# A graph layer's edge loop: constants in a PSUM bank, one-hots on ScalarE, four engines ordered by hand, and a start and end shared differently

## The chip, the cores and the metric

One core of a Trainium2 chip runs the whole program. Its engines work side by side, each through its own list of instructions, and wait for each other by semaphores: TensorE (PE in the profile; its weight loads are PEld), VectorE (DVE), ScalarE (ACT), GpSimd (POOL) and SyncE (SP), which here only issues transfers. The metric is the device time of one execution in microseconds. The profile is of one execution, whose time is given beside its span.

## The reference

A layer of a graph network on 12,500 nodes of 32 features and 400,000 edges, which come sorted by their destination `dst`:

```python
h = jnp.maximum(_layernorm(x), 0.0)                          # 12500 x 32
e_feat = jnp.concatenate([h[src], h[dst], edge_attr], -1)     # 400000 x 96
v = jax.nn.relu(e_feat @ W1 + b1) @ W2 + b2                   # 96 -> 64 -> 32
out = x + jnp.maximum(segment_max(v, dst, 12500), h)
```

The layer norm divides by `sqrt(var + 1e-5)` and has no weights. The sources are random, so `h[src]` is a true gather of 400,000 rows of 128 bytes; the destinations are sorted, so consecutive edges mostly share theirs.

## The kernel before

**Start.** Partition p holds nodes 98p to 98p+97 (`NT` is 98). `x` is normalized in four pieces of 28, 28, 28 and 14 nodes per partition (L155 to L174), reductions and scaling on VectorE, squares and roots on ScalarE, and `h` is stored to `h_d` in DRAM (L174). From `h` come also `hs` (L209, L210), its value in two parts for TensorE, and the table `q_d`, h times the destination part of W1 (L222 to L232). A stage named "windows" (L236 to L268) works out for each edge whether it is the last of its destination (`at`), and a flag for inputs that the fast path can't take (then the code from L433 on runs; it doesn't here).

**The loop.** The edges lie in four stripes of 196 chunks of 512. The loop (L363 on; 98 iterations) takes two chunks of all four stripes, a *pair*, at a time. Per pair:

- *Sources.* A chunk needs `h[src]` for 16 blocks of 128 edges. Twelve are fetched by GpSimd with one indirect DMA each (L143). Four (`MM`) are made on TensorE, in *tiles*: VectorE builds one-hot matrices `hot` and `its` from keys (L285, L287); 15 matmuls (L292, L295) select the rows, with a large negative penalty on all but the wanted one of 14 nodes; VectorE's max-reduction (L297) takes it into `gm`. Chunks 0, 1 and 195 have no tiles and are gathered whole. `to_features` (L324, L326) transposes both kinds into `ht`. The tiles come from a generator, one per `next(tiles)`, one pair ahead of their use.
- *Hidden layer.* Four PSUM banks `ph0` to `ph3`, one per stripe, sum up three products (L379): of the edge attributes `ea`, of the destination part, and of `ht` with w1a. The destination part is a window `qw` of 32 rows of `q_d`, loaded from the chunk's first destination on, times a one-hot `of` that VectorE builds from the destinations (L370). ScalarE's relu gives `hid` (L389).
- *Output and maximum.* w2 (L399) puts two chunks into two `pv` banks; VectorE's scan (L404) runs the maximum along the edges, reset by penalties `pb` where the destination changes. In the *leave* of a chunk, `leave_1` transposes the scan (L336), adds b2 (`so`, L338) and marks the last edge of each destination (`last`, L340); `leave_2` brings these edges' values into node order by matmul (L350), ScalarE copies them (`wo`, L353), and SyncE stores them to `top_d` (L357).

**Banks and buffers.** PSUM: `ph0` to `ph3`, `tr` for the leaves, and three `pv` banks, which the tiles and w2 share in turn. Gathered chunks have six buffers, so GpSimd may run three pairs ahead: the gathers of a pair wait until the transposes of the pair three before have freed its buffers.

**Order.** In the loop SyncE and TensorE follow the order of the code; VectorE, ScalarE and GpSimd are ordered by a scheduler, which places the transposes into `ht` of the next pair ahead of the rest of the present one: in the trace L324 stands, one iteration early, after the reduction of the present iteration's first tile.

**End.** Both `top_d` and `h` are loaded, the maximum and the sum with `x` are taken in four pieces (L423 to L429, L507, L508) and stored.

Of the kernel before, what the change touches and what calls it, by code (L numbers as in the profile page):

```python
# [20 lines left out]
DVE = mybir.EngineType.DVE  # L21

# [21 lines left out]
MMC = range(2, NCH - 1)  # L44
AHEAD = 2
PIECE = 2 * A0
ROUND = 12582912.0
# [11 lines left out]
def gnn_kernel(ctx, tc, x, src, src_mm, src_t, dst, dst_next, dst_ext, lo, hi, edge_attr, weights, w1, w2, b2, out):  # L59
# [41 lines left out]
    lo_i = const.tile([1, NS, NCH], I32, name="lo_i")  # L101
    nc.sync.dma_start(lo_i, lo.rearrange("(o s) c -> o s c", o=1))
# [6 lines left out]
    node = const.tile([P, NCH], F32, name="node")  # L109
    for s in range(NS):  # L110
        nc.gpsimd.iota(node[s * W:(s + 1) * W], pattern=[[0, NCH]], base=0, channel_multiplier=1,
                       allow_small_or_imprecise_dtypes=True)
# [36 lines left out]
    with tc.tile_pool(name="nodes", bufs=1) as pool, tc.tile_pool(name="nodes_ps", bufs=2, space=PSUM) as ps:  # L149
# [4 lines left out]
        sts = [pool.tile([P, 2, PIECE], F32, name=f"st{k}") for k in range(len(pieces))]  # L154
        with tc.manual_schedule(engines={DVE, SP}):  # L155
            for st, r in zip(sts, pieces):
                n = r.stop - r.start
                nc.vector.tensor_reduce(st[:, 0, :n], xs[:, r], axis=AX.X, op=ALU.add)
                nc.vector.tensor_scalar(st[:, 0, :n], st[:, 0, :n], 1.0 / D, None, op0=ALU.mult)
                nc.vector.tensor_tensor(h[:, r], xs[:, r], st[:, 0, :n, None].to_broadcast([P, n, D]),  # L160
                                        op=ALU.subtract)
                nc.scalar.activation(sq[:, r], h[:, r], AF.Square)
            for st, r in zip(sts, pieces):
                n = r.stop - r.start
                nc.vector.tensor_reduce(st[:, 1, :n], sq[:, r], axis=AX.X, op=ALU.add)
                nc.vector.tensor_scalar(st[:, 1, :n], st[:, 1, :n], 1.0 / D, EPS, op0=ALU.mult, op1=ALU.add)
                nc.scalar.activation(st[:, 0, :n], st[:, 1, :n], AF.Sqrt)
            for st, r in zip(sts, pieces):
                n = r.stop - r.start
                nc.vector.reciprocal(st[:, 1, :n], st[:, 0, :n])  # L170
                nc.vector.scalar_tensor_tensor(h[:, r], h[:, r], 0.0,
                                               st[:, 1, :n, None].to_broadcast([P, n, D]),
                                               op0=ALU.max, op1=ALU.mult)
                nc.sync.dma_start(h_v[:, r], h[:, r])  # L174
# [39 lines left out]
        nc.vector.tensor_tensor(node, node, lo_w, op=ALU.add)  # L214
# [57 lines left out]
    with tc.tile_pool(name="edges", bufs=3) as pool, tc.tile_pool(name="edges_ps", bufs=1, space=PSUM) as ps, \  # L272
            tc.manual_schedule(engines={SP, PE}):
        loaded = {}
        windows = {}
        mm_rows = {}

        def rows_by_matmul():

            for i, c in enumerate(MMC):  # L280
                kb = pool.tile([P, 2, MM * P], F16, name="kb", bufs=2)
                nc.scalar.dma_start(kb, ap(key_d, i * MM * P, [[0, P], [len(MMC) * MM * P, 2], [1, MM * P]]))
                hot = pool.tile([P, A1, MM * P], F32R, name="hot", bufs=2)
                for k in range(A1):
                    nc.vector.tensor_scalar(hot[:, k], kb[:, 0], key_p[:, k:k + 1], None, op0=ALU.is_equal)  # L285
                its = pool.tile([P, MM * P], BF16, name="its", bufs=2)
                nc.vector.tensor_scalar(its, kb[:, 1], place, None, op0=ALU.is_equal)  # L287
                gm = mm_rows[c] = pool.tile([P, MM, D], F32, name="gm", bufs=6)
                for m in range(MM):
                    e = slice(m * P, (m + 1) * P)  # L290
                    po = ps.tile([P, C], F32, name="pv", bufs=3)[:, :D * A0]
                    nc.tensor.matmul(po, its[:, e], others.rearrange("p f a -> p (f a)"), start=True, stop=False)  # L292
                    for k in range(A1):
                        for part in range(2):
                            nc.tensor.matmul(po, hot[:, k, e], hs[:, part, k].rearrange("p f a -> p (f a)"),  # L295
                                             start=False, stop=(k == A1 - 1 and part == 1))
                    nc.vector.tensor_reduce(gm[:, m, :], po.rearrange("p (f a) -> p f a", a=A0),  # L297
                                            axis=AX.X, op=ALU.max)
                    yield

        def load(c):
            if c % LOAD == 0:
# [5 lines left out]
                for s in range(NS):  # L308
                    g = slice(s * D, (s + 1) * D)
                    nc.scalar.dma_start(db[g, :n], ap(dst_ext, 1 + s * S + c * C, [[0, D], [1, n]]))  # L310
                    nc.scalar.dma_start(pb[g, :n], ap(pen_d, s * S + c * C, [[0, D], [1, n]]))
                for k in range(c, min(c + LOAD, NCH)):
                    loaded[k] = [t[:, (k - c) * C:(k - c + 1) * C] for t in (ea, db, pb)]
            _, base = nc.values_load_multi_w_load_instructions(
                lo_i[0:1, :, c], engines=[SP], min_val=0, max_val=N)
            qw = pool.tile([P, HID], F32, name="qw", bufs=6)
            for s in range(NS):
                nc.sync.dma_start(qw[s * W:(s + 1) * W, :], q_d[bass.ds(base[s], W), :])
            windows[c] = qw, base
# [11 lines left out]

        def leave_1(c, sm):

            px = ps.tile([P, J, P], F32, name="tr")
            for j in range(J):
# [3 lines left out]
            last = pool.tile([P, J, NS, W], F32, name="last", bufs=2)  # L339
            nc.vector.tensor_tensor(  # L340
                last, iota_w[:, None, None, :].to_broadcast([P, J, NS, W]),
                at[:, :, c * J:(c + 1) * J].rearrange("p s j -> p j s")[:, :, :, None].to_broadcast([P, J, NS, W]),
                op=ALU.is_equal)
            return so, last

        def leave_2(c, so, last):

            pw = ps.tile([P, J, P], F32, name="tr")[:, 0]
            for j in range(J):
                nc.tensor.matmul(pw, last[:, j].rearrange("p s w -> p (s w)"), so[:, j, :],  # L350
                                 start=(j == 0), stop=(j == J - 1))
            wo = pool.tile([P, P], F32, name="wo")
            nc.scalar.activation(wo, pw, AF.Copy)  # L353
            _, base = windows.pop(c)
            for s in range(NS):
                g = slice(s * W, (s + 1) * W)
                nc.sync.dma_start(top_d[s % 2][bass.ds(base[s], W), :], wo[g, s * D:(s + 1) * D])  # L357

        tiles = rows_by_matmul()
        for c in range(AHEAD):  # L360
            load(c)
        sm = None
        for c in range(0, NCH, 2):  # L363
            for k in range(c + AHEAD, min(c + AHEAD + 2, NCH)):
                load(k)
            gh = [gather(c + x) for x in range(2)]
            of = []
            for x in range(2):
                of.append(pool.tile([P, C], F32, name="of", bufs=4))
                nc.vector.tensor_scalar(of[x], loaded[c + x][1], node[:, c + x:c + x + 1], None, op0=ALU.is_equal)  # L370


            ph = [ps.tile([P, C], F32, name=f"ph{s}") for s in range(NS)]

            def into_ph(pairs, start, stop):
                for s in range(NS):
                    g = slice(s * D, (s + 1) * D)
                    for x, (w, e) in enumerate(pairs):
                        nc.tensor.matmul(ph[s][x * HID:(x + 1) * HID], w[g], e[g], start=start, stop=stop)  # L379

            into_ph([(w1c, loaded[c + x][0]) for x in range(2)], True, False)
            into_ph([(windows[c + x][0], of[x]) for x in range(2)], False, False)
            next(tiles, None)
            ht = [to_features(c + x, gh[x]) for x in range(2)]
            into_ph([(w1a, ht[x]) for x in range(2)], False, True)
# [4 lines left out]
            next(tiles, None)  # L390
            next(tiles, None)

            if c > 0:
                left = leave_1(c - 1, sm)
            pv = [ps.tile([P, C], F32, name="pv", bufs=3) for x in range(2)]
            for s in range(NS):
                for x in range(2):
                    g = slice(x * HID, (x + 1) * HID)
                    nc.tensor.matmul(pv[x][s * D:(s + 1) * D], w2x[g], hid[s][g], start=True, stop=True)  # L399
            sms = []  # L400
            for x in range(2):
                before = -LOW if sm is None else sm[:, C - 1:C]
                sm = pool.tile([P, C], F32, name="sm", bufs=4)
                nc.vector.tensor_tensor_scan(sm, loaded.pop(c + x)[2], pv[x], before, op0=ALU.add, op1=ALU.max)  # L404
                sms.append(sm)
            next(tiles, None)
            next(tiles, None)
            if c > 0:
                leave_2(c - 1, *left)
            next(tiles, None)  # L410
            left = leave_1(c, sms[0])
            next(tiles, None)
            leave_2(c, *left)
# [157 lines left out]
```

## Time and profile before

| what | value |
|---|---|
| median of three runs (lowest, highest) | 5231.67 us (5231.43, 5264.13) |
| profiled execution: time, span | 5227.3 us, 5225.5 us |
| mean granted TensorE clock | 0.81 |
| busy: TensorE, its weight loads, VectorE, ScalarE, GpSimd | 70%, 53%, 35%, 6%, 43% |
| gathers (L143) | 2353, of 950 ns each |
| tile matmuls (L292, L295), reductions (L297) | 772 + 10808, 772 of 623 ns |
| first gather, first w2, last w2's end, end | 29.7, 232.8, 5184.9, 5225.5 us |

How to read it: an engine's busy time is only of its work on data; its waiting is given as idle time ahead of an instruction, with the last to release it ("<-DVE ht L324" means that VectorE's instruction of line 324, which writes `ht`, ended the wait; "issue" means that nothing which the profile shows was waited for, and "remote" a signal of another engine). A group's row has the count, the busy time in sum, the mean of one in nanoseconds, and the idle time. A shape such as 128x448 is partitions by elements. A window's row gives the busy time of each engine within a stretch of the span, the number of instructions, and the granted clock as a share of full speed.

### The profile page before, as it was taken

To read this page: it belongs to the slowest core of one execution; us is meant where nothing else is said; L and a number is where in the kernel's file an instruction comes from. 1 tells how busy PE (TensorE), PEld (TensorE's weight loads), DVE (VectorE), ACT (ScalarE), POOL (GpSimd) and SP (SyncE) were. 2 spreads that over 40 slices of the span, in tenths; PEclk is the share of its full clock that TensorE was granted. 3 is DMA by queue.
4 is the path that set the end of the run, shared out by engine and by line. 5 is a ranking of instruction groups with operands and counts; after the bars stand their busy time and mean duration, and the time that the engine had idled before them with its cause. 6 is when DMAs were issued, how large, how long until landed. Compare 5 with 4: busy or idle time off the path is not lost. (4 is left out here: it accounts for less than half of the span.)

```text
span 5225.5 us, 57318 instructions
## 1 busy us (share of the span) xinstructions
PE 3638.2 (70%) x20281; PEld 2775.9 (53%) x20281; DVE 1846.3 (35%) x3612; ACT 315.6 (6%) x627; POOL 2238.9 (43%) x2369
## 2 busy tenths in 40 slices
PE   2376767676767676767676767676767676777687
PEld 1255555555555555555554555555555555555565
DVE  2333333333333333333333333333333333333344
ACT  1000000000000000000000000000000000000000
POOL 6534344444444444444444444444444444444420
PEclk6587878787878787878788888787878787878788
DMA  3321112211211121112111211121112211211121
GB/s 123 90 58 43 42 39 58 44 41 40 58 42 41 40 56 44 40 40 56 44 40 40 57 44 40 40 56 44 41 40 57 44 41 40 57 44 40 40 53 65
DMA packets 235577, 256.47 MB, mean 49 GB/s; under 512 B 123653, under 2 KB 211861, under 8 KB 222102
## 3 DMA queue, kind: packets, MB, share of 16 engines
q10 hardware_dynamic: 74084, 137.60, 9.7%
q0 software_dynamic: 75296, 38.70, 5.6%
q1 hardware_dynamic: 85906, 76.48, 4.9%
q8 instruction: 159, 2.61, 0.2%
q14 instruction: 132, 1.08, 0.1%
HBM read 238.44 MB, written 14.04 MB: 48 GB/s over the span
## 5 line engine op out<-in xcount | busy, mean ns | idle before, releaser
L143 POOL DMA_INDIRECT gh<-h_d,src_i x2353 | 2234.8, 950 | 2812.1 <-DVE ht L324 2098.3
L295 PE MATMUL pv<-hs,hot 128*128 128x448 f32 x10808 | 2874.0, 413 | 712.6 <-issue 712.4
L295 PEld LDWEIGHTS pv<-hs,hot 128*128 128x128 f32 x10808 | 2282.8, 212 | 1444.9 <-issue 1270.9
L297 DVE TENSOR_REDUCE gm<-pv 128x32 f32<-128x448 f32 x772 | 481.2, 623 | 2548.3 <-remote 1529.4
L292 PE MATMUL pv<-others,its 128*128 128x448 bf16 x772 | 301.9, 391 | 427.0 <-issue 386.0
L285 DVE TENSOR_SCALAR hot<-kb,key_p 128x512 fp32r<-128x512 f16 x1351 | 555.8, 479 | 9.5 <-DMA qw<-q_d 9.5
L350 PE MATMUL tr<-so,last 128*128 128x128 f32 x1568 | 250.2, 282 | 250.0 <-issue 240.8
L404 DVE TENSOR_TENSOR_SCAN sm<-pb,sm,pv 128x512 f32<-128x512 bf16 x195 | 248.9, 1276 | 469.3 <-remote 332.5
L350 PEld LDWEIGHTS tr<-so,last 128*128 128x128 f32 x1568 | 227.1, 197 | 229.5 <-issue 211.8
L389 ACT ACTIVATE hid<-ph,wt 128x512 f32<-128x512 f32 x392 | 239.3, 690 | 973.5 <-PE ph L379 529.9
L292 PEld LDWEIGHTS <-its 128*128 128x128 bf16 x772 | 78.0, 101 | 400.5 <-issue 387.4
L353 ACT ACTIVATE wo<-tr 128x128 f32<-128x128 f32 x196 | 54.5, 278 | 3810.7 <-remote 1817.6
L336 PE MATMUL tr<-ident,sm 128*128 128x128 f32 x784 | 146.0, 319 | 22.3 <-ACT wo L353 22.3
L336 PEld LDWEIGHTS tr<-ident,sm 128*128 128x128 f32 x784 | 117.9, 167 | 57.9 <-ACT wo L353 38.4
L338 DVE TENSOR_TENSOR so<-tr,wt 128x512 f32<-128x512 f32 x196 | 133.9, 683 | 24.1 <-PE pv L292 11.5
L340 DVE TENSOR_TENSOR last<-iota_w,at 128x512 f32<-128x512 f32 x196 | 131.6, 672 | 28.2 <-PE tr L350 28.2
L324 DVE STREAM_TRANSPOSE ht<-gh 128x384 f32<-128x384 f32 (+1 forms) x196 | 102.9, 563 | 71.0 <-PE ph L379 54.8
L379 PE MATMUL ph<-ea,wt 32*64 32x512 f32 x1568 | 110.0, 617 | 8.4 <-DMA ea<-in_edge_attr 8.4
L379 PE MATMUL ph<-ht,wt 32*64 32x512 f32 x1568 | 110.9, 612 | 0.5 <-issue 0.4
L379 PE MATMUL ph<-of,qw 32*64 32x512 f32 x1568 | 105.5, 592 | 6.2 <-issue 6.2
L399 PE MATMUL pv<-hid,wt 64*32 64x512 f32 x1568 | 108.9, 604 | 0.2 <-ACT hid L389 0.2
L287 DVE TENSOR_SCALAR its<-kb,place 128x512 bf16<-128x512 f16 x193 | 69.6, 361 | 96.4 <-remote 80.1
(68 smaller groups left out, 399.3 us busy)
## 6 DMA issues: line engine op xcount, KB each, us to landing
ea<-in_edge_attr SPq DMA_DIRECT2D x49, 1024.0 KB
db<-in_dst_ext ACTq DMA_DIRECT2D x196, 256.0 KB
kb<-key_d ACTq DMA_DIRECT2D x193, 256.0 KB
gh<-h_d,src_i POOLq DMA_INDIRECT x2353
pb<-pen_d ACTq DMA_DIRECT2D x196, 128.0 KB
qw<-q_d SPq DMA_DIRECT2D x784, 8.0 KB
top_d<-wo SPq DMA_DIRECT2D x784, 4.0 KB
top_d<-zero ACTq DMA_DIRECT2D x2, 1568.0 KB
```

The lines of the kernel that those rows point to most:

```text
L143: nc.gpsimd.indirect_dma_start(out=gh[:, k, :], out_offset=None, in_=h_d[:, :], in_offset=bass.IndirectOffsetOnAxis(ap=src_i[:, c, k:k + 1 ...
L285: nc.vector.tensor_scalar(hot[:, k], kb[:, 0], key_p[:, k:k + 1], None, op0=ALU.is_equal)
L292: nc.tensor.matmul(po, its[:, e], others.rearrange("p f a -> p (f a)"), start=True, stop=False)
L295: nc.tensor.matmul(po, hot[:, k, e], hs[:, part, k].rearrange("p f a -> p (f a)"), start=False, stop=(k == A1 - 1 and part == 1))
L297: nc.vector.tensor_reduce(gm[:, m, :], po.rearrange("p (f a) -> p f a", a=A0), axis=AX.X, op=ALU.max)
L336: nc.tensor.transpose(px[:, j, :], sm[:, j * P:(j + 1) * P], ident)
L338: nc.vector.tensor_tensor(so, px, b2r[:, None, :].to_broadcast([P, J, P]), op=ALU.add)
L340: nc.vector.tensor_tensor(last, iota_w[:, None, None, :].to_broadcast([P, J, NS, W]), at[:, :, c * J:(c + 1) * J].rearrange("p s j -> p j ...
L350: nc.tensor.matmul(pw, last[:, j].rearrange("p s w -> p (s w)"), so[:, j, :], start=(j == 0), stop=(j == J - 1))
L379: nc.tensor.matmul(ph[s][x * HID:(x + 1) * HID], w[g], e[g], start=start, stop=stop)
L389: nc.scalar.activation(hid[s], ph[s], AF.Relu, bias=b1c)
L404: nc.vector.tensor_tensor_scan(sm, loaded.pop(c + x)[2], pv[x], before, op0=ALU.add, op1=ALU.max)
```

## The change

All of these are made together.

- *Start*: GpSimd normalizes one of the four pieces (28 of 98 nodes), with pairwise additions in place of the reduction. On VectorE the mean's scale goes into one operation with the subtraction, and on ScalarE scale and eps go into the root.
- *Tiles* are made for chunks 0 and 1 too, ahead of the loop: 780 in place of 772, and 2345 gathers in place of 2353.
- *Constants and one-hots*: `last` reads its row of numbers from a PSUM bank, `iota_ps`; for it `pv` has two banks, not three. `of` is made by ScalarE in two operations, relu(1 - (dst - node)^2).
- *Leave*: `leave_2` does its product in two groups of 64 columns, 16 matmuls in place of the 8 that the trace counts for one leave; `top` and `wo` are 64 wide.
- *Transfers*: `db` and `pb` take one DMA each in place of four; keys come for two chunks at once; first destinations of two chunks are read in one go, without a bounds check; loads run four chunks ahead, not two; `qw` has 8 buffers, `sm` and `of` 3.
- *Order*: VectorE and ScalarE are ordered by hand too. An iteration is: transposes into `ht`, w1a, relu; then ScalarE's one-hots for the next pair; tiles 0 to 2 of the next pair's first chunk, the next pair's `ea` products, w2, the next pair's windows, the leave of the odd chunk of the iteration before, and the other five tiles, with the leaves between them.
- *End*: `h` is summed on GpSimd from the parts in `hs`, not loaded from `h_d`.

```diff
-MMC = range(2, NCH - 1)
-AHEAD = 2
+MMC = range(NCH - 1)
+AHEAD = 4
+GP = 1
...
+        shares = [(nc.vector, st, r) for st, r in zip(sts, pieces)]
+        shares.append((nc.gpsimd, *shares.pop(GP)[1:]))
+        def total(v, out, of):
+            if v is nc.vector:
+                v.tensor_reduce(out, of, axis=AX.X, op=ALU.add)
+                return
+            k = D // 2
+            v.tensor_tensor(half, of[:, :, :k], of[:, :, k:], op=ALU.add)
+            while k > 2:
+                k //= 2
+                v.tensor_tensor(half[:, :, :k], half[:, :, :k], half[:, :, k:2 * k], op=ALU.add)
+            v.tensor_tensor(out[:, :, None], half[:, :, 0:1], half[:, :, 1:2], op=ALU.add)
...
+                total(v, st[:, 0, :n], xs[:, r])
+                if v is nc.vector:
+                    v.scalar_tensor_tensor(h[:, r], mean, -1.0 / D, xs[:, r], op0=ALU.mult, op1=ALU.add)
+                else:
+                    v.tensor_scalar(st[:, 0, :n], st[:, 0, :n], 1.0 / D, None, op0=ALU.mult)
+                    v.tensor_tensor(h[:, r], xs[:, r], mean, op=ALU.subtract)
...
+                nc.scalar.activation(st[:, 0, :n], st[:, 1, :n], AF.Sqrt, scale=1.0 / D, bias=eps)
...
-            tc.manual_schedule(engines={SP, PE}):
+            tc.manual_schedule(engines={SP, PE, DVE, ACT}):
+        iota_ps = ps.tile([P, C], F32, name="iota_ps")[:, :W]
+        nc.vector.tensor_copy(iota_ps, iota_w)
...
-                    po = ps.tile([P, C], F32, name="pv", bufs=3)[:, :D * A0]
+            po = ps.tile([P, C], F32, name="pv", bufs=2)[:, :D * A0]
...
-                for s in range(NS):
-                    g = slice(s * D, (s + 1) * D)
-                    nc.scalar.dma_start(db[g, :n], ap(dst_ext, 1 + s * S + c * C, [[0, D], [1, n]]))
-                    nc.scalar.dma_start(pb[g, :n], ap(pen_d, s * S + c * C, [[0, D], [1, n]]))
+                nc.scalar.dma_start(db[:, :n], ap(dst_ext, 1 + c * C, [[S, NS], [0, D], [1, n]]))
+                nc.scalar.dma_start(pb[:, :n], ap(pen_d, c * C, [[S, NS], [0, D], [1, n]]))
...
-                nc.vector.tensor_scalar(of[x], loaded[c + x][1], node[:, c + x:c + x + 1], None, op0=ALU.is_equal)
+        def window_hots(c):
+            of = ofs[c] = pool.tile([P, C], F32, name="of", bufs=3)
+            nc.scalar.activation(of, loaded[c][1], AF.Square, bias=below[:, c:c + 1])
+            nc.scalar.activation(of, of, AF.Relu, bias=ones, scale=-1.0)
...
-                nc.tensor.matmul(pw, last[:, j].rearrange("p s w -> p (s w)"), so[:, j, :],
-                                 start=(j == 0), stop=(j == J - 1))
+                for g in range(2):
+                    nc.tensor.matmul(pw[g * 2 * W:(g + 1) * 2 * W],
+                                     last[:, j, 2 * g:2 * g + 2].rearrange("p s w -> p (s w)"),
+                                     so[:, j, g * 2 * D:(g + 1) * 2 * D], start=(j == 0), stop=(j == J - 1))
...
         for c in range(0, NCH, 2):
+            a, b = c + 2, c + 3
+            gh = [gather(c + x) for x in range(2)]
+            load_keys(a + 2)
             for k in range(c + AHEAD, min(c + AHEAD + 2, NCH)):
                 load(k)
             ht = [to_features(c + x, gh[x]) for x in range(2)]
+            into_ph(ph, [(w1a, ht[x]) for x in range(2)], False, True)
             hid = []
             for s in range(NS):
                 hid.append(pool.tile([P, C], F32, name="hid", bufs=6))
                 nc.scalar.activation(hid[s], ph[s], AF.Relu, bias=b1c)
+            for k in range(a, min(a + 2, NCH)):
+                window_hots(k)
+            tile(a, 0)
+            one_hots(b, range(3))
+            tile(a, 1)
+            one_hots(b, range(3, A1))
+            last = [lasts(c)]
+            tile(a, 2)
+            ph = edges_into(a)
...
+            windows_into(a, ph)
+            leave()
...
+            tile(a, 3)
+            so = leave_1(c, sms[0])
+            last.append(lasts(c + 1))
+            tile(b, 0)
+            one_hots(a + 2, range(4))
+            leave_2(c, so, last[0])
+            tile(b, 1)
+            so = leave_1(c + 1, sms[1])
+            one_hots(a + 2, range(4, A1))
+            tile(b, 2)
+            tile(b, 3)
+            leave = lambda c=c + 1, so=so, last=last[1]: leave_2(c, so, last)
...
+        nc.gpsimd.tensor_tensor(h.rearrange("p (g a) f -> p g a f", a=A0),
+                                hs[:, 0].rearrange("p g f a -> p g a f"),
+                                hs[:, 1].rearrange("p g f a -> p g a f"), op=ALU.add)
...
-        for r in pieces:
-            nc.sync.dma_start(h[:, r], h_v[:, r])
```

## The prediction

> **What bounds the kernel now.** I read the page's first two parts, then its groups, the windows of single loop iterations, the timeline inside one, and the chain of waits. TensorE is busiest, but only 70%:
>
> ```profile
> PE 3638.2 (70%) x20281; PEld 2775.9 (53%) x20281; DVE 1846.3 (35%) x3612; ACT 315.6 (6%) x627; POOL 2238.9 (43%) x2369
> L143 POOL DMA_INDIRECT gh<-h_d,src_i x2353 | 2234.8, 950 | 2812.1 <-DVE ht L324 2098.3
> L295 PE MATMUL pv<-hs,hot 128*128 128x448 f32 x10808 | 2874.0, 413 | 712.6 <-issue 712.4
> L297 DVE TENSOR_REDUCE gm<-pv 128x32 f32<-128x448 f32 x772 | 481.2, 623 | 2548.3 <-remote 1529.4
> ```
>
> GpSimd waits 2098 us for VectorE's transposes (buffers come free), VectorE's reductions wait 1529 us for something "remote" (TensorE's signals), TensorE for its own issue. The loop handles two chunks (a pair) per iteration, 98 in all; windows compare one iteration without gathers (first row, near the end) with pieces of one with them (columns: us; PE, PEld, DVE, ACT, POOL busy; granted clock; DMA share; GB/s):
>
> ```profile
> 5111.00:5142.20 31.20, 31.20 (x213) 25.33 (x212) 18.30 (x38) 2.98 (x6) 0.00 (x0) 1.00 0.17 47
> 2521.50:2527.50 6.00, 6.00 (x43) 4.92 (x44) 1.64 (x4) 1.42 (x3) 4.74 (x5) 1.00 0.10 16
> 2527.50:2553.20 25.70, 12.42 (x62) 8.52 (x46) 3.23 (x4) 0.00 (x0) 17.98 (x19) 0.77 0.10 13
> 2553.20:2572.70 19.50, 17.90 (x119) 14.07 (x120) 13.55 (x30) 1.73 (x5) 0.16 (x1) 0.87 0.31 98
> ```
>
> An iteration of pure TensorE work is **31.2 us**, PE full and clock 1.0. With gathers it is 51.2 us here, and 52.2 on average: bursts start 92 intervals apart from 231.4 to 5030.8 us (4799.4/92). So **the toll of the gathers is 21 us a pair**, some 2000 us of the span. The timeline shows where it lies:
>
> ```profile
> 2521.50 0.95 POOL L143 DMA_INDIRECT gh<-h_d,src_i  x1 [23.02 <-DVE ht L324]
> 2526.68 0.62 DVE L297 TENSOR_REDUCE gm<-pv 128x32 f32<-128x448 f32 x1 [2.46 <-PE pv L295]
> ...
> 2553.24 0.62 DVE L297 TENSOR_REDUCE gm<-pv 128x32 f32<-128x448 f32 x1 [18.08 <-remote]
> ```
> ```profile
> 2528.07 3.13 PE L295 MATMUL pv<-hs,hot 128*128 128x448 f32 x14
> 2532.86 3.13 PE L295 MATMUL pv<-hs,hot 128*128 128x448 f32 x14
> ...
> 2541.33 1.24 PE L295 MATMUL pv<-hs,hot 128*128 128x448 f32 x2 [1.08 <-issue]
> 2544.13 0.53 PE L295 MATMUL pv<-hs,hot 128*128 128x448 f32 x1 [1.57 <-issue]
> ```
>
> All 24 gathers of a pair are issued in one burst, 1.25 us apart, 2521.5 to 2551.2, then GpSimd idles 21 us till the next transposes. For the burst's first 6 us all is normal. Then TensorE issues a matmul only every 1.4 us or so, and its completions come late: the tile that ends about 2531 is reduced at 2553.24, two microseconds after the last gather. In that crawl TensorE does what was not waiting for VectorE; all else comes after it. The start shows the same with almost nothing else running: between 82 and 100 us, with gathers back to back, a node-table step that takes VectorE 0.29 us waits 8.11 us.
>
> ```profile
> 91.16 0.29 DVE L227 COPY ht<-hp 128x128 f32<-128x128 f32 x1 [8.11 <-remote]
> 92.58 0.42 PE L225 MATMUL hp<-ident,h 128*64 128x128 f32 x1
> 99.55 0.29 DVE L227 COPY ht<-hp 128x128 f32<-128x128 f32 x1 [8.11 <-issue]
> ```
>
> So a period is: the burst with its crawl (31.7 us, 2521.5 to 2553.2) plus what TensorE could not do in it (19.4 us).
>
> **The change, part by part.**
>
> *Order of an iteration* (decides the sum). Before, the transposes `ht` for the next pair run one iteration ahead (L324 at 2571.69, inside other TensorE work), and three `pv` banks let TensorE run on past late reductions. Between 2521.5 and 2553.2 it got through nearly all of four tiles (15 matmuls, 3.05 us each), w2 and half a leave. After, `ht` is made at the head of its own iteration, the tiles of the next pair follow, and `pv` has two banks, which w2 shares with the tiles. Two costs follow.
>
> (a) A bubble. The last tile's reduction 0.62, the transposes of the first chunk 0.55 + 0.30, then w1a's first half: 1.4 us, and the second chunk's transposes some 0.8 more: TensorE idles about 2.1 us, bounds 1.4 and 2.3 (all four transposes and the reduction, less signals). An undisturbed iteration becomes 33.3.
>
> (b) The burst starts with these transposes, so TensorE meets the crawl with w1a, tile (a,0) and a part of (a,1) done: 1.06 + 3.05 + about 1.5 of the first 6 us. In the crawl (25.7 us at 1.4 us a matmul, some 18) it ends (a,1), (a,2) and perhaps the ea matmuls, then stands at w2, which needs the `pv` banks of (a,1) and (a,2): their reductions come when the crawl ends, 31.7 + some 1.0 for the signal and first reduction + 0.65 for the second: 33.4 us. Behind w2 in TensorE's queue stand: w2 itself 1.05, of 0.95, leave 1.06, five tiles 15.25, two leave transposes 1.1, leave 1.06 = 20.5; then reduction and transposes to the next burst 1.3; and the clock, 0.5 in the crawl and 1.0 again only after about 4 us of work, costs 2.0 (an estimate from the third and fourth rows, 0.77 and 0.87). Period: 33.4 + 20.5 + 1.3 + 2.0 = **57.2 us**. The same counting gives the 51.2 seen before (31.7 + 19.5).
>
> *Leave in column groups.* 16 matmuls of 64x64 for 8 records of L350 (0.9 to 1.05 us a leave). By w2's 0.066 each it is 1.06, the same; by L350's own 0.111 it is 1.78. Half the column work at half the price would save 0.45. Per pair -0.9 to +1.5; I take 0, nearest w2, as the tiles are equally narrow.
>
> *One-hots to ScalarE, `last` from PSUM.* VectorE loses two `of` a pair (2 x 0.48) and ScalarE gains four operations of some 0.6 (from hid's 690 ns). Both lie in idle time: VectorE is 35% busy, ScalarE 6%. Nothing.
>
> *Hidden:* one DMA for four of db and pb, one for two of kb, four windows and stores as before, one base load per pair on SP, deeper `qw`: transfers are at a share of 0.10 to 0.31, and no long wait on them stands in the chain. If cover went, a load at 3 us (kb at the start) would cost 3 a pair; I put 0.
>
> *Tiles for chunks 0 and 1:* 8 tiles more (24.4 us at clock 1.0), 8 gathers fewer (10 us of GpSimd).
>
> *Start.* VectorE sheds one 28-node piece and small operations, some 6 us; GpSimd does that piece's 4452 elements per partition at between 0.95 and 2.76 ns (its memset and iota rows), 4.2 to 12.3 us, beside VectorE. First gather (29.7 us before) moves by -5 to +5; I take -3. Then 72 gathers (90 us), not 80, with the same crawling table, the windows' work to about 159, then by hand: key load 3.5, eight one-hots 3.1, four tiles at half clock 15, one-hots 3.7, four tiles 13, one-hots 3.7: 42 us. First burst of the loop at 203 (195 to 215).
>
> The Trainium skill, "GPSIMD Engine Reference", section "3.1 Elementwise — side-by-side cycle accounting", gives 4497 ns for an add of 2048 elements; by it the piece is an estimated 9.8 us, inside those bounds, and nothing in the sum moves by more than 3 us.
>
> *End.* From the last, partial burst of 17 gathers: 48.7 (57.2 less 7 x 1.25) + 33.3 + 21 (four tiles fewer) + 13 (none) + 25 (28.4 now, the reload of h gone): 141. GpSimd's sum of h, 3136 elements, 3 to 8.7 us, lies beside the loads.
>
> **Sum.** 94 periods lie between first and last burst: 203 + 94 x 57.2 + 141 = **5720**, against the profiled execution's 5227.3; the median shown, 5231.67, is 4 above that, within what a forecast like this can tell.
>
> **Rivals.**
> B, *the toll is a fixed 21 us wherever TensorE stands.* For: bursts at different places in the iteration have much the same toll (51 to 53). Against: TensorE's banks decide what it does in the crawl. 33.3 + 21 = 54.3: 5450; with the bubble at 1.6 and the leave's saving, 5310.
> C, *the burst meets work as good as before's:* (a,1), (a,2), ea done early and the signals not as late; the bubble hides in the crawl. 52.2: 5250.
> D, *faster: the toll goes.* Then GpSimd's descriptors and VectorE's operands disturb each other, and taking `of` and `last`'s constant off the VectorE path cures it: 33.3 a pair, 203 + 3130 + 126, 3460. It wins from a period below 52.0 ((5227 - 344)/94), a toll below 18.7. Against: the one-hots stay on VectorE, and in the crawl VectorE is idle 22 of 25.7 us while the gathers keep their 1.25; an operation that isn't there can't be the cause.
>
> The Trainium skill, "SBUF — State Buffer", section "Who interferes with whom", says that only VectorE and GpSimd share a port and "PE and ACT never wait on anyone." By that rule no burst slows TensorE, and the changed kernel would take the 33.3 of rival D; the rows at 2541 to 2553 and at 91 to 99 us contradict it, and I go by them.
>
> **Chances.** Forecast 0.60 (5550 to 5870: the leave +1.5 a pair, start +12; bubble and crawl work -1.8), B 0.20, C 0.07, D 0.13. The range 5310 to 5870 holds the first two. About 1% is what a measurement here tells from no change; C is that. Faster 0.13, same 0.07, slower 0.80.
>
> **What would show it.** In the changed kernel's profile: bursts 57 us apart; TensorE idle about 2 us ahead of each w1a (L424), ended by a transpose; w2 (L480) starting 33 us after the burst's first gather, its wait ended by a reduction (L347) that was idle some 20 us; last iterations without gathers at 33.3; the first burst of the loop near 203. Wrong, if w2 runs inside the crawl, if reductions are not late, or if gathers come in another rhythm than 24 at 1.25 us.

## The result, and the profile after

| | before | changed |
|---|---|---|
| median of four runs each, us | 5238.3 | 5648.38 |
| lowest to highest | 5231.43 to 5264.13 | 5643.08 to 5669.14 |
| profiled execution's span | 5225.5 | 5650.3 |

The changed kernel is slower: the ratio is 1.078, 95% interval 1.0733 to 1.0828. 5720 was forecast.

From the page of the changed kernel, engines first, then the groups that answer to those shown of before (busy, mean ns, idle time ahead and what ended it):

```profile
PE 3811.8 (67%) x21969; PEld 2609.1 (46%) x21969; DVE 1787.1 (32%) x3431; ACT 564.9 (10%) x1019; POOL 2289.4 (41%) x2377
L145 POOL DMA_INDIRECT gh<-h_d,src_i x2345 | 2260.5, 964 | 3241.0 <-DVE ht L382 2549.8
L347 DVE TENSOR_REDUCE gm<-pv 128x32 f32<-128x448 f32 x780 | 487.2, 625 | 3184.8 <-PE pv L344 1572.6
L480 PE MATMUL pv<-hid,wt 64*32 64x512 f32 x1568 | 300.0, 989 | 1421.7 <-DVE gm L347 885.8
```

VectorE sheds 59 us and ScalarE takes on 249, as the moved one-hots should do; both stay idle for most of the span. The new line is the last: w2, which before waited for next to nothing (0.2 us in all), now waits 1422 us. The same group in the page of before:

```profile
L399 PE MATMUL pv<-hid,wt 64*32 64x512 f32 x1568 | 108.9, 604 | 0.2 <-ACT hid L389 0.2
```

Windows of the changed kernel, an iteration without gathers first, then one with them in three pieces (us; PE, PEld, DVE, ACT, POOL busy; granted clock; DMA share; GB/s):

```profile
5561.40:5595.90 34.50, 33.10 (x233) 25.32 (x228) 14.31 (x26) 5.54 (x10) 0.00 (x0) 0.95 0.01 2
2505.60:2511.60 6.00, 5.96 (x37) 4.19 (x38) 1.63 (x4) 4.17 (x7) 4.72 (x5) 1.00 0.07 11
2511.60:2538.60 27.00, 12.73 (x61) 5.72 (x61) 4.72 (x11) 0.93 (x2) 18.46 (x19) 0.69 0.09 13
2538.60:2562.40 23.80, 22.30 (x128) 17.51 (x126) 11.25 (x21) 0.45 (x2) 0.00 (x0) 0.85 0.20 50
```

The first row holds 34.5 where before had 31.2; the last piece holds 23.8 where before had 19.5. In that iteration, from its timelines on VectorE and TensorE:

```profile
2516.99 0.62 DVE L347 TENSOR_REDUCE gm<-pv 128x32 f32<-128x448 f32 x1 [4.37 <-PE pv L344]
...
2531.12 0.62 DVE L347 TENSOR_REDUCE gm<-pv 128x32 f32<-128x448 f32 x1 [11.06 <-remote]
```
```profile
2505.64 1.76 PE L424 MATMUL ph<-ht,wt 32*64 32x512 f32 x16 [1.40 <-DVE ht L382]
...
2513.46 3.20 PE L344 MATMUL pv<-hs,hot 128*128 128x448 f32 x14
...
2531.81 1.95 PE L480 MATMUL pv<-hid,wt 64*32 64x512 f32 x14 [12.12 <-DVE gm L347]
```

w1a (L424) starts after a bubble of 1.40 us. The tile that ends about 2516.6 is reduced only at 2531.12, and w2, but for the first two of its 16 matmuls, stands waiting for that reduction. The chain that was forecast is thus there to be seen; the experiments ask how much of the loss is its doing.

| term | forecast | measured |
|---|---|---|
| first burst of the loop | 203 | 191.8 |
| 94 periods of | 57.2 | 56.5 (54.9 to 58.3) |
| from the last burst to the end | 141 | 147.6 |
| span | 5720 | 5650.3 |

### The profile page after: what moved, and what is told of

Its sections match the earlier page's. It is cut to its first block, busy times and chain, and to the rows that moved or that the text cites. A ratio compares the mean times of both kernels' runs of the same rounds, so it can differ in the third digit from the quotient of the medians.

```text
span 5650.3 us, 58413 instructions
## 1 busy us (share of the span) xinstructions
PE 3811.8 (67%) x21969; PEld 2609.1 (46%) x21969; DVE 1787.1 (32%) x3431; ACT 564.9 (10%) x1019; POOL 2289.4 (41%) x2377
## 5 line engine op out<-in xcount | busy, mean ns | idle before, releaser
L344 PE MATMUL pv<-hs,hot 128*128 128x448 f32 x10920 | 2540.3, 388 | 0.0
L344 PEld LDWEIGHTS pv<-hs,hot 128*128 128x128 f32 x10920 | 2145.5, 197 | 168.7
L480 PE MATMUL pv<-hid,wt 64*32 64x512 f32 x1568 | 300.0, 989 | 1421.7 <-DVE gm L347 885.8
L424 PE MATMUL ph<-of,qw 32*64 32x512 f32 x1568 | 436.7, 1050 | 98.8 <-issue 97.3
L424 PEld LDWEIGHTS ph<-of,qw 32*64 32x64 f32 x1568 | 86.9, 192 | 452.5 <-issue 451.9
L424 PE MATMUL ph<-ht,wt 32*64 32x512 f32 x1568 | 180.7, 647 | 138.8 <-DVE ht L382 138.8
L410 PEld LDWEIGHTS tr<-so,last 128*64 128x64 f32 x3136 | 138.5, 172 | 185.6 <-issue 180.4
L410 PE MATMUL tr<-so,last 128*64 128x64 f32 x3136 | 169.2, 266 | 2.8 <-DVE so L402 2.8
L374 ACT ACTIVATE of<-db,below 128x512 f32<-128x512 int32 x196 | 141.7, 723 | 61.3 <-DMA db<-in_dst_ext 61.3
L424 PEld LDWEIGHTS ph<-ht,wt 32*64 32x64 f32 x1568 | 41.1, 131 | 221.1 <-DVE ht L382 220.7
L375 ACT ACTIVATE of<-of,ones 128x512 f32<-128x512 f32 x196 | 142.0, 725 | 6.4
L424 PE MATMUL ph<-ea,wt 32*64 32x512 f32 x1568 | 134.7, 612 | 11.1 <-issue 10.4
```

Of the source, the lines that this page charges most:

```text
L374: nc.scalar.activation(of, loaded[c][1], AF.Square, bias=below[:, c:c + 1])
L375: nc.scalar.activation(of, of, AF.Relu, bias=ones, scale=-1.0)
L410: nc.tensor.matmul(pw[g * 2 * W:(g + 1) * 2 * W], last[:, j, 2 * g:2 * g + 2].rearrange("p s w -> p (s w)"), so[:, j, g * 2 * D:(g + 1) * ...
```

## The experiments

One plain fact has to come first: **chips differ.** The kernel before took 3190 to 3196 us in 20 runs on two chips and 5216 to 5342 us in 14 runs on two others, of the kind on which the first profile was taken. Each run below is compared with the kernel before on its own chip; "quick" and "slow" name the two kinds of chip. A run's chip could not be chosen, and three of the four chips were met at one time only, so that it is the chip, and not something else that holds for some minutes, is the simplest reading and not shown.

### The changed kernel without gathers, and as it is, on a quick chip

```diff
+    first = []
...
 def gather(c):
-    gh = gathered.tile([P, K, D], F32, name="gh")
+    if first:
+        return first[0]
+    gh = const.tile([P, K, D], F32, name="gh")
+    first.append(gh)
```

> The changed kernel with its gathers left out but for the first chunk's, whose rows every chunk reads: the output is not the layer's, all other work is the same. If gathers are what lengthens the iteration and the rest is TensorE's work and the bubble of 2.1 us: 33.3 us an iteration, total 3350 to 3500. If the bubble would be hidden: 31.2 and 3150 to 3250. If the toll comes from elsewhere: over 5000.

> The changed kernel unaltered, beside the kernel before on this chip. Where gathers slow TensorE (kernel before near 5230): 5640 to 5670. Where they don't (kernel before near 3190): the bubble at the iteration's head alone decides, 34.5 us an iteration against 31.2, 3470 to 3490. If the two pv banks cost something without the crawl as well: over 3500.

Without gathers: 3476.92 us. As it is: 3479.66, ratio 1.0903 (1.0883 to 1.0922). Where there is no crawl (the slow issue of the prediction's timeline), 2300 gathers cost 3 us, which is within what runs differ by, and the change costs 287 us all the same. The loop of the kernel as it is has two kinds of iterations there, 27 of 95 of 33.0 us and the others of 34.5; one of each, TensorE's timeline:

```profile
2011.54 1.76 PE L424 MATMUL ph<-ht,wt 32*64 32x512 f32 x16 [1.40 <-DVE ht L382]
...
2013.27 3.13 PE L344 MATMUL pv<-hs,hot 128*128 128x448 f32 x14
```
```profile
2044.51 1.91 PE L424 MATMUL ph<-ht,wt 32*64 32x512 f32 x16 [1.39 <-DVE ht L382]
...
2046.39 4.57 PE L344 MATMUL pv<-hs,hot 128*128 128x448 f32 x14
```

The bubble is the same in both. Behind the second one the first tile takes 4.57 us, not 3.13; a window over its first part has a granted clock of 0.67, where the other's has 1.00:

```profile
2013.20:2016.20 3.00, 3.00 (x22) 2.65 (x15) 0.00 (x0) 2.91 (x5) 2.39 (x3) 1.00 0.15 21
2045.00:2048.00 3.00, 3.00 (x21) 1.72 (x20) 0.11 (x1) 1.63 (x3) 2.37 (x3) 0.67 1.06 204
```

So a bubble of 1.4 us costs some 2.1 us by itself (1.40 and 0.7 in w1a, whose second half waits for the second chunk's transposes), and in about three iterations of four some 1.5 us of clock besides. 33.3 was forecast without that, and 34.1 is the mean.

Which iterations lose the clock can be read from the trace too. All its changes of the clock lie whole multiples of 3.41 us apart, as if at the ticks of a fixed grid. The bubble of the slower iteration begins at 2043.12, 0.5 us behind such a tick; the three steps from there on:

```profile
2042.59:2046.00 3.41, 2.02 (x19) 0.57 (x17) 1.96 (x5) 0.00 (x0) 1.16 (x2) 1.00 0.85 183
2046.00:2049.41 3.41, 3.41 (x16) 2.72 (x10) 0.00 (x0) 3.03 (x5) 2.62 (x3) 0.50 0.95 165
2049.42:2052.83 3.41, 3.41 (x19) 2.98 (x18) 1.81 (x4) 2.06 (x3) 2.69 (x3) 1.00 0.39 97
```

The other bubble begins 1.7 us behind a tick and loses nothing. Over the whole loop, 70 of the 71 bubbles that begin less than 1.4 us behind a tick are followed by one step at 0.50, and none of the 26 that begin later.

### The first tile ahead of w1a

```diff
             ht = [to_features(c + x, gh[x]) for x in range(2)]
+            tile(a, 0)
             into_ph(ph, [(w1a, ht[x]) for x in range(2)], False, True)
...
-            tile(a, 0)
             one_hots(b, range(3))
```

> The changed kernel with one line moved: TensorE does the next pair's first tile before w1a, not after, so that VectorE's reduction and four transposes lie beside that tile, as in the kernel before. Theory (the bubble and the slow clock behind it are the whole loss where gathers cost nothing): there 34.5 -> 30.5 to 31.0 us an iteration, total 3080 to 3140, under the kernel before. Where gathers slow TensorE: the bubble's 2 to 4 us go, the late w2 stays, total 5300 to 5480. Rival (the loss lies in ScalarE's one-hots or the column groups): 3450 to 3490, or 5630 to 5670.

On a quick chip 3163.49 us, ratio **0.9914** (0.9896 to 0.9932). This one line turns the change there from 9.0% slower to 0.9% faster. The iteration is full (window of one, and w1a in it):

```profile
1997.00:2027.80 30.80, 30.80 (x232) 24.22 (x224) 17.53 (x34) 5.54 (x10) 23.47 (x24) 1.00 0.23 58
```
```profile
2019.64 1.11 PE L424 MATMUL ph<-ht,wt 32*64 32x512 f32 x16
```

The iteration is as expected, 30.8; the total is 23 us over the expected range, because what lies around the loop was put too short: the first w2 comes at 150.1 us, the last ends 39 us ahead of the end. The rivals, ScalarE's one-hots and the column groups, are still in this kernel, and so are not the loss on a quick chip. The clock bears the reading out: in this kernel it stays at 1.00 all through the loop.

### Three banks, two banks

```diff
-        iota_ps = ps.tile([P, C], F32, name="iota_ps")[:, :W]
-        nc.vector.tensor_copy(iota_ps, iota_w)
+        iota_ps = iota_w
...
-            po = ps.tile([P, C], F32, name="pv", bufs=2)[:, :D * A0]
+            po = ps.tile([P, C], F32, name="pv", bufs=3)[:, :D * A0]
...
-            pv = [ps.tile([P, C], F32, name="pv", bufs=2) for x in range(2)]
+            pv = [ps.tile([P, C], F32, name="pv", bufs=3) for x in range(2)]
```

> The changed kernel with three pv banks again; the constant of the last-edge mark is read from SBUF, nothing else differs. Theory 1 (two banks make w2 wait for reductions whose signals come late): w2 moves from about 29 us after the burst's first gather to about 13, the fourth tile from 37 to about 30, period 56.5 -> 50 to 52 us, total 5050 to 5250. Theory 2 (a burst costs a fixed 21 us wherever TensorE stands, and the changed kernel adds only its bubble): period stays 56.5, total 5630 to 5670.

> The kernel before with two pv banks instead of three (the bank is left empty). Theory 1: w2 stays near 6 us after the burst's start, but the tile that starts 22 us in must wait for a reduction at about 32 us; one tile less within the burst, period 52.0 -> 55 to 56 us, total 5500 to 5620. Theory 2: 5220 to 5260.

Both came to a quick chip, where neither theory's numbers apply. The changed kernel with three banks: 3477.09, ratio 1.0886 (1.0867 to 1.0905), so there its two banks cost nothing. The kernel before with two (the same edit the other way, without the constant): 3375.16, ratio 1.0568 (1.0551 to 1.0586). In its order the tile behind w2 needs the bank that the scan still reads, 1.4 us in 97 iterations, 139 of the 183 us that it lost (its waits: us in total, times, longest):

```profile
PE pv L292 <- DVE sm L404: 139.3, 97, 1.5
```

So whether a third bank matters depends on the order of the work. For iterations without a crawl the prediction did not consider it.

### w2 early, three banks, w1a at the head, on a slow chip

```diff
             tile(a, 0)
+            pv = [ps.tile([P, C], F32, name="pv", bufs=3) for x in range(2)]
+            for s in range(NS):
+                for x in range(2):
+                    g = slice(x * HID, (x + 1) * HID)
+                    nc.tensor.matmul(pv[x][s * D:(s + 1) * D], w2x[g], hid[s][g], start=True, stop=True)
...
+                nc.vector.tensor_tensor_scan(sm, loaded.pop(c + x)[2], pv[x], before, op0=ALU.add, op1=ALU.max)
+                sms.append(sm)
             one_hots(b, range(3))
             tile(a, 1)
```

The same lines are gone from behind `tile(a, 2)` and `edges_into(a)`, and the constant is in SBUF as in the section above.

> The changed kernel with three pv banks (constant in SBUF) and with w2 and the scans right after the next pair's first tile, not after the third and the ea products; w1a stays at the head with its bubble. Where the kernel before takes near 3190: the bubble is the whole loss there and stays, so 3470 to 3490, ratio 1.087 to 1.093; if w2's place matters there too, off that by over 1%. Where it takes over 5000: if the late w2 is what the changed kernel lost to the crawl, w2 within 7 us of the burst's first gather, 52 to 53.5 us an iteration, ratio 0.99 to 1.02; if not, 1.07 to 1.08 as the changed kernel.

5713.15 us, ratio **1.0854** (1.0802 to 1.0905), on a slow chip: no better than the changed kernel's 1.078. On average w2 (by its third matmul, as two can run ahead of the wait) now starts 5.2 us after the burst's first gather, where it was 29.0 in the changed kernel, and it waits for next to nothing, 0.7 us in all; the period is 57.2 us. So **the late w2 was not the loss.** TensorE's timeline shows what takes its place:

```profile
2481.07 1.09 PE L473 MATMUL pv<-hid,wt 64*32 64x512 f32 x16
...
2487.54 4.71 PE L343 MATMUL pv<-hs,hot 128*128 128x448 f32 x14
2492.18 1.60 PE L423 MATMUL ph<-ea,wt 32*64 32x512 f32 x6
2495.30 0.98 PE L423 MATMUL ph<-ea,wt 32*64 32x512 f32 x1 [1.52 <-issue]
2497.39 1.01 PE L423 MATMUL ph<-ea,wt 32*64 32x512 f32 x1 [1.12 <-issue]
2499.49 1.01 PE L423 MATMUL ph<-ea,wt 32*64 32x512 f32 x1 [1.09 <-issue]
```

The ea products (16 in 1.1 us elsewhere) now crawl, one in 2 us. Counting TensorE's matmuls by the trace, in the 92 or 94 periods between the loop's bursts in each run on a slow chip, on average:

| kernel | matmuls from the burst's first gather to 33 us | of these at 6 to 33 us | of those in tiles | tile matmuls left after 33 us | period |
|---|---|---|---|---|---|
| before | 88.4 | 46.6 | 36.6 | 59.2 | 52.2 |
| before, another slow chip | 84.5 | 42.9 | 33.1 | 62.8 | 53.1 |
| changed | 89.6 | 54.7 | 25.1 | 75.0 | 56.5 |
| changed, w2 early, three banks | 90.2 | 46.4 | 28.8 | 75.0 | 57.2 |
| changed, first tile ahead of w1a (two forms below) | 88.7, 89.2 | 48.3, 49.2 | 12.6, 13.0 | 83.0 | 56.4, 57.1 |

By 33 us all of them have begun about as many matmuls, 85 to 90, of whatever kind. That holds for the changed kernel too, whose TensorE runs on undisturbed for some 12 us and then stands at w2. Before, three quarters or more of those at 6 to 33 us are tile matmuls of 0.2 us each; in all forms of the changed kernel the ea, w2 and window products, each 16 matmuls in 1.1 us when undisturbed, stand ahead of the remaining tiles and take up that stretch's places. 15.8 tile matmuls more (75.0 less 59.2) at 0.203 are 3.2 us of the 4.3 by which the period grew; the bubble, which lies behind the crawl, has 1.4 us of idle time. That it is the kind of matmul that decides rests on these counts and is not shown: a kernel made to put only tiles into the crawl was not run, and on a slow chip the one-hots on ScalarE and the transfers were never taken back.

### The same with the first tile ahead: the leave in one group, the normalization on VectorE

```diff
-                for g in range(2):
-                    nc.tensor.matmul(pw[g * 2 * W:(g + 1) * 2 * W],
-                                     last[:, j, 2 * g:2 * g + 2].rearrange("p s w -> p (s w)"),
-                                     so[:, j, g * 2 * D:(g + 1) * 2 * D], start=(j == 0), stop=(j == J - 1))
+                nc.tensor.matmul(pw, last[:, j].rearrange("p s w -> p (s w)"), so[:, j, :],
+                                 start=(j == 0), stop=(j == J - 1))
...
```
```diff
-        shares.append((nc.gpsimd, *shares.pop(GP)[1:]))
```

> The changed kernel with the first tile before w1a, and the leave's product in one group of 128 columns again, 64 wide parts of it stored as before. Where gathers cost nothing: the 16 small matmuls took 0.69 us a leave, the 8 large ones 1.05, so 0.36 x 196 = 70 us more than the kernel with the first tile moved (3163), 3220 to 3245. By the prediction's value (column groups change nothing): 3150 to 3175.

> The changed kernel with the first tile before w1a, and all four pieces normalized by VectorE again (scale and eps stay folded). By the prediction's value (GpSimd's share brings the first full burst forward by about 3 us) where gathers cost nothing: 3160 to 3172. If GpSimd's own chain is what holds up the first gathers: first gather earlier than 27 us or total below 3160. If VectorE was the bound: 5 us or more above 3163.

> The kernel before unaltered, for a trace of it on this chip. Where its time is near 3190: gathers still issued 1.25 us apart, but VectorE's reductions not late and TensorE issuing without pause, 31.2 us an iteration as in the last iterations of the first trace. Where it is near 5230: the late reductions and the crawl of the first trace, 52 us.

These three came to one slow chip. The kernel before: 5321.68, with the late reductions and 53.1 us a period. With the leave in one group 5732.05, ratio 1.0758 (1.0732 to 1.0783); with all pieces on VectorE 5654.9, ratio 1.0609 (1.0586 to 1.0633). Both have the first tile ahead of w1a, and against 1.078 for the changed kernel that is worth at most two per cent here, not nine: taking the bubble away helps little on a slow chip, as the tile matmuls that it moves out of the crawl (83.0 left in the table, not 75.0: 1.6 us) take back most of what it gives. The second differs from the first in both edits; their periods differ by 0.76 us (57.13, 56.37), which fits the leave: 0.36 a leave, two a pair, 0.72. The first burst of the loop comes at 200.4 us with GpSimd's share and at 214.0 without, on the same chip: 14 us for that part of the change, not 3, though the first gather was issued at 27.2 with it and 28.5 without. The traces show where it comes from: with GpSimd's share TensorE begins on the node table at 17.1 us, without it at 20.4, and the table's last step ends at 113.1 against 128.3. The 3 us that were forecast are there, but they lie ahead of the first gathers, and steps that are done by then are spared the crawl; the prediction's rows show two that waited 8.11 us in it.

### Both moves and three banks, twice on quick chips

> As the run with the first tile before w1a, and besides three pv banks (the constant in SBUF again), with w2 and the scans right after the second tile, not after the third and the ea products: the kernel before's order around the burst. Where gathers cost nothing: as that run, 3080 to 3140. Where they slow TensorE: w2 runs before the crawl sets in, four tiles lie within the burst, 51 to 52 us an iteration, total 5100 to 5220, under the kernel before. If a burst costs a fixed toll: no difference from the run with only the first tile moved.

> The kernel with the first tile before w1a, three pv banks, and w2 and the scans right after the second tile, once more, for a chip on which the kernel before takes over 5000 us. There, if the late w2 is what the changed kernel lost: w2 within 10 us of the burst's first gather, not near 29, 51 to 52.5 us an iteration, a ratio of 0.97 to 1.00 to the kernel before. If a burst's toll is fixed, or what was lost lies elsewhere: 55 us or more, a ratio over 1.05, as the kernel with the first tile moved (1.061). Where the kernel before takes near 3190: 3205 to 3215 again, which tells nothing new.

3210.59 and 3213.33 us, ratios 1.0056 (1.0038 to 1.0074) and 1.0062 (1.0045 to 1.0079): 1.5% behind the kernel with only the first tile moved, which was not expected. With iterations of 30.8 us the gathers are at their own bound: GpSimd issues all the loop's gathers without a pause, and they take 1022 ns on average, 980 with only the tile moved. With 0.30 between them, 24 are 31.7 and 30.7 us. VectorE now waits for landings (its wait: us in total, times, longest):

```profile
DVE ht L379 <- DMA gh<-h_d,src_i: 62.8, 24, 6.9
```

The question that it was meant for, the order around a burst on a slow chip, it never met.

### Gathers spaced out: an experiment that failed

```diff
                     in_offset=bass.IndirectOffsetOnAxis(ap=src_i[:, c, k:k + 1], axis=0))
+                nc.gpsimd.memset(filler, 0.0)
...
```

> The kernel before with a small memset on GpSimd after each gather, so that gathers are issued about every 1.55 us and not every 1.25; nothing is left out. If TensorE crawls because gathers come faster than something drains them (the first five of a burst disturb nothing): no late reductions, period near the longer burst, 39 to 42 us, total 4000 to 4300. If each gather slows TensorE whatever the distance: the crawl lasts as long as the longer burst, period 52 to 55 us, total 5200 to 5550.

4080.57 us on a quick chip, but the gathers were not spaced: GpSimd's order was left to the scheduler, which put up to 36 memsets in a row (from GpSimd's timeline).

```profile
1715.01 14.78 POOL L147 MEMSET filler<- 128x256 f32 x36
```

The run shows what these memsets cost and says nothing of the crawl.

## Why the prediction was right, and which step of it failed

- *The sum.* 57.2 a period was forecast and 56.5 measured, 203 and 191.8 to the first burst, 141 and 147.6 behind the last: the total fell 1.3% below the forecast, inside the range and inside the likeliest case's own. In part that is luck: the errors at the two ends have opposite signs, and the period came out though one step of its working failed, (b) below.
- *The toll* of a burst as what bounds both kernels: right for the chip of the profile, and shown by the last iterations of either trace. As far as these runs show, it is a property of some chips, which no view of one trace could tell.
- *(a), the bubble*: right in kind and in the size of its own part, 2.1. The term left out is the clock behind it: where nothing else disturbs, most bubbles cost 3.7 (34.5 less 30.8), not 2.1.
- *(b), "then stands at w2, which needs the `pv` banks"*: the step that failed. The wait was there, and ended a few microseconds earlier than forecast (29.0, not 33.4). But freeing w2 of it, banks and order both, gave back nothing (57.2 a period, not less than 56.5). The sum still came out, because in its place the light products crawl: with w2 late or early, five tiles (75.0 matmuls) are left over when the crawl ends. What was right was the count of tiles left; what was wrong is that the wait for the banks left them. What does is argued from the counts above; why TensorE crawls at all stays open.
- *Column groups, taken as no change*: the 16 matmuls take 0.69 us where the 8 took 1.05, so they save 0.36 a leave, 0.72 a pair, inside the bounds of -0.9 to +1.5.
- *One-hots on ScalarE and the constant in PSUM, taken as nothing*: agrees with the kernel that keeps both and is faster than before on a quick chip.
- *Start*: GpSimd's share moved the first burst by 14 us on a slow chip, not by 3; its chain took 14 us of GpSimd's time within 5.5 to 23.6 us, just over the bound of 12.3. *End*: of the sum's terms, 48.7 should be 48.45 (57.2 less 7 x 1.25), which matters little; from the last w1a to the end it took 44.1 us, not 13 and 25. From the end of the last w2 it is 37.7 us, as before (37.8: that w2 ends at 5187.7, not at 5184.9 as the table of before has it). So taking out the reload of h gained nothing: the sum of parts on GpSimd took 11.3 us, not 3 to 8.7, and the first of VectorE's maxima (L516), which runs beside it, took 7.67 us, where none took over 1.09 before.
- *Rivals.* B, a fixed toll of 21 us, would have been 54.3, and C, work as good as before's beside the burst, 52.2: too low for every changed form on a slow chip. D, the toll goes: it does, on quick chips, with 3480 us against D's 3460, but for the kernel before as well, so it is no gain. Its cause as D had it, operands of VectorE and GpSimd, is not supported: neither kernel was altered between the two kinds of chip.

## What to carry to other kernels

When a stretch of the trace issues about the same number of instructions whatever their size, look at which instructions lie in it: by the counts above, long ones there and short ones for when issue is free would be the better order, though no run has tried it. Moving the last producer of an input next to its consumer can cost more than the wait that is seen, since TensorE's clock fell behind it in three iterations of four; one tile between the two, the same work in another order, was worth 9% on a quick chip, and at most two on a slow one. And before an explanation that rests on a wait is believed, take that wait away: here the wait was real, was long, and was not the loss.

## What the runs showed of the hardware

- The same program takes 3193 us on some chips and 5230 to 5330 on others. On the slow ones TensorE begins only 43 to 55 matmuls from 6 to 33 us into a burst of indirect gathers (an undisturbed iteration has 213 in 31.2 us), and reductions come up to some 25 us after their tile's last matmul, while gathers keep their 1.25 us. On quick chips TensorE is full beside a stream of gathers without a pause. What differs between the chips stays open: gathers are issued alike, and the median packet of their queue took 42 to 44 ns in traces of either kind.
- In these traces the granted clock changes only at ticks 3.41 us apart. A TensorE pause of 1.4 us with another 0.7 soon behind it cost one such step at 0.50 in 70 of 71 cases where it began less than 1.4 us behind a tick, and in none of 26 where it began later (the changed kernel on a quick chip); the iterations are 34.5 us long in the first case and 33.0 in the second.
- An elementwise VectorE operation of 128x896 that takes 1.09 us took 7.67 beside a GpSimd operation of 11.3 us, at the end of the changed kernel.
- On quick chips the gathers, at 0.98 to 1.02 us each with 0.30 between, are the next bound: 24 of them are 30.7 to 31.7 us, TensorE's work 30.8.
